# One group in 42 of a gather fetched row by row by SyncE, at byte offsets from registers

## The chip, the cores and the metric

The kernel runs on one core of one Trainium2 chip. A core has a matrix engine (TensorE, PE in the profile), a vector engine (VectorE, DVE), a scalar engine (ScalarE, ACT), a general engine (GpSimd, POOL) and a synchronising engine (SyncE, SP), each with its own list of instructions, and 16 DMA engines that all of them share. The metric is the device time of one execution in microseconds (us), the median of several runs.

## The reference

The kernel scores 16384 users of a recommender. There are 50001 items. For every item two attention steps over 32 neighbours give two vectors of 32 numbers; with a looked-up row of 64 they make the item's row of 128. Each user has a history of 100 items and one target item:

```python
a_sus = _neighbor_attn(E_in, near_full)        # 50001 x 32: softmax over 32 neighbours
a_inf = _neighbor_attn(E_out, near_full)
h = concat([E_hist[history], a_sus[history], a_inf[history]])   # 16384 x 100 x 128
t = concat([E_tgt[target], a_inf[target], a_sus[target]])       # 16384 x 128
z = relu(einsum('bld,hd->blh', h * t[:, None, :], W1) + b1)
exp_A = exp(einsum('blh,h->bl', z, W2[0])) * ((history != target[:, None]) & (history != 0))
attn = exp_A / sum(exp_A, axis=-1, keepdims) ** 0.5
s = sum(h * attn[..., None])                   # one number over everything
out = sigmoid(cosine(s broadcast, t))
```

The row of `h` for every user and every history position, 1,638,400 rows of 128 numbers, has to be looked up by index. That look-up is what the change is about.

## The kernel before

The kernel has two stages, one after the other.

The first stage computes the item rows. It takes the items in 391 sub-tiles of 128 (23 blocks of 17; the names `NITER`, `NSUB`), gathers the 32 neighbours of each with 32 indirect DMAs on POOL (line 136, tile `v`), does the attention on DVE and ACT, and writes the rows to two tables in memory: `table` with the history version and `ttab` with the target version. A row of `table` has `W` = 129 numbers, 516 bytes: the sum of the row first, so that it need not be computed again, then the 128 numbers.

The second stage, the user stage, takes the 16384 users in `UC` = 128 chunks of 128, one user to a partition. The 100 history positions of a chunk are worked in `NG` = 25 groups of `LG` = 4 positions. The steps of the loop are numbered `s` = 25 c + g, 3200 in all. The functions are:

- `history_of(i)` (line 290): SP loads the history numbers of four chunks (`BSUB`) into a tile `hidx`; four such tiles exist (`u_in`).
- `target_rows(c)` (line 294): one indirect DMA on POOL gathers the 128 target rows of a chunk; `target_work(c)` (line 304) turns them with PE and builds the mask on DVE.
- `gather(s)` (line 325): four indirect DMAs on POOL (line 332) gather the four rows of each of the 128 users, one position at a time, into a tile `h` of 128 x 4 x 129; there are `HBUF` = 20 of these.
- `turn(s)` (line 342): PE turns the four 128 x 128 blocks (line 346) into a PSUM tile `hT_ps`, of which there are three.
- `times_target(s)` (line 348): DVE multiplies by the target rows (line 351) and copies the four row sums aside (line 354).
- `hidden(s)`, three steps later: PE multiplies by `w1T` (line 363), ACT applies relu (line 365).
- `scored(s)`, six steps later: PE multiplies by the one row of W2 (line 372), adding up the 25 groups of a chunk in one PSUM tile.
- `kept`, `turned_back`, `weights`, `ended`: once for each chunk, exponentials, mask and sums.

In this stage the order of the work on all five engines is the order in which the program calls these functions (`tc.manual_schedule`). Each engine runs its own instructions in that order and waits on semaphores for what it needs. POOL can run ahead of PE by as many groups as there are `h` tiles. SP has 32 history lists to load in this stage and, at the end, one result to write. A `history_of` call stands at the third chunk of a list and loads the next one:

```python
if g == 0 and c % BSUB == 2 and 0 < c // BSUB and c // BSUB + 1 < UC // BSUB:
    history_of(c // BSUB + 1)
```

An indirect DMA of POOL takes one index per partition from a tile on the core and fetches 128 rows. A DMA of SP, as used before, moves a block whose place in memory is fixed when the program is built.

Of the kernel before, what the change touches and what calls it, by code (L numbers as in the profile page):

```python
# [10 lines left out]
F32 = mybir.dt.float32  # L11
I32 = mybir.dt.int32
U8 = mybir.dt.uint8
E = mybir.EngineType
AF = mybir.ActivationFunctionType
ALU = mybir.AluOpType
AX = mybir.AxisListType

P = 128
ITEMS = 50001  # L20
# [21 lines left out]
UC = B // P  # L42
BSUB = 4
LG = 4
NG = L // LG
W = 1 + D
LAG = 3
HBUF = 20

@with_exitstack
def kernel(
# [13 lines left out]
    nc = tc.nc  # L67
# [8 lines left out]
    table = dram.tile([ROWS, W], F32, name="table")  # L76
# [3 lines left out]
    ident = const.tile([P, P], F32, name="ident")  # L80
# [25 lines left out]
    with (  # L106
# [7 lines left out]
        its = {}  # L114
# [15 lines left out]
        def gather(s):  # L130
            it, j = divmod(s, NSUB)
            nidx = its[it][0]
            v = n_v.tile([P, K, 2, G], F32, name="v")
            subs[s].update(v=v)
            for k in range(K):
                nc.gpsimd.indirect_dma_start(  # L136
                    out=v[:, k].rearrange("p t d -> p (t d)"),
                    out_offset=None,
                    in_=egeo,
                    in_offset=bass.IndirectOffsetOnAxis(ap=nidx[:, j, k : k + 1], axis=0),  # L140
                )
# [128 lines left out]
    with (  # L270
# [2 lines left out]
        tc.tile_pool(name="u_in", bufs=4) as u_in,  # L273
        tc.tile_pool(name="u_t", bufs=3) as u_t,
        tc.tile_pool(name="u_h", bufs=HBUF) as u_h,
        tc.tile_pool(name="u_x", bufs=6) as u_x,
        tc.tile_pool(name="u_z", bufs=6) as u_z,
        tc.tile_pool(name="u_s", bufs=3) as u_s,
# [8 lines left out]
        users, hists = {}, {}  # L287
        rows, got, hT, xT, z = {}, {}, {}, {}, {}

        def history_of(i):  # L290
            hists[i] = u_in.tile([P, BSUB, L], I32, name="hidx")
            nc.sync.dma_start(hists[i], hist_v[i])

        def target_rows(c):
            t = u_t.tile([P, D], F32, name="t")
            nc.gpsimd.indirect_dma_start(  # L296
                out=t,
                out_offset=None,
                in_=ttab[0:ITEMS, :],
                in_offset=bass.IndirectOffsetOnAxis(ap=tidx[:, c : c + 1], axis=0),  # L300
            )
            users[c] = {"t": t, "hidx": hists[c // BSUB][:, c % BSUB, :]}

        def target_work(c):
            u = users[c]
            t = u["t"]
            tT_ps = ps_t.tile([P, LG, P], F32, name="hT_ps")
            nc.tensor.transpose(tT_ps[:, 0, :], t, ident)  # L308
            tT = u_t.tile([D, 1, P], F32, name="tT")
            nc.vector.tensor_copy(tT[:, 0, :], tT_ps[:, 0, :])  # L310
            u["tT"] = tT
            nc.vector.tensor_reduce(tsum[:, c : c + 1], t, AX.X, ALU.add)
            junk = u_t.tile([P, D], F32, name="junk")
            nc.scalar.activation(junk, t, AF.Square, accum_out=tsq[:, c : c + 1])
            keep = u_s.tile([P, L], F32, name="keep")
            idf = u_s.tile([P, L], F32, name="idf")
            nc.vector.tensor_copy(idf, u["hidx"])
            nc.vector.tensor_scalar(keep, idf, 0.0, None, ALU.not_equal)
            nc.vector.scalar_tensor_tensor(
                keep, idf, tidf[:, c : c + 1], keep, ALU.not_equal, ALU.mult  # L320
            )
            u["keep"] = keep
            u["hsum"] = u_s.tile([P, L], F32, name="hsum")

        def gather(s):
            c, g = divmod(s, NG)
            rows[s] = u_h.tile([P, LG, W], F32, name="h")
            got[s] = []
            for q in range(LG):
                l = g * LG + q  # L330
                got[s].append(
                    nc.gpsimd.indirect_dma_start(  # L332
                        out=rows[s][:, q, :],
                        out_offset=None,
                        in_=table,
                        in_offset=bass.IndirectOffsetOnAxis(
                            ap=users[c]["hidx"][:, l : l + 1], axis=0
                        ),
                    )
                )  # L340

        def turn(s):
            c, g = divmod(s, NG)
            hT[s] = ps_t.tile([P, LG, P], F32, name="hT_ps")
            for q in range(LG):
                nc.tensor.transpose(hT[s][:, q, :], rows[s][:, q, 1:W], ident)  # L346

        def times_target(s):
            c, g = divmod(s, NG)
            xT[s] = u_x.tile([D, LG, P], F32, name="xT")  # L350
            nc.vector.tensor_tensor(  # L351
                xT[s], hT.pop(s), users[c]["tT"].to_broadcast([D, LG, P]), ALU.mult
            )
            copy = nc.vector.tensor_copy(  # L354
                users[c]["hsum"][:, g * LG : (g + 1) * LG],
                rows.pop(s)[:, :, 0:1].rearrange("p q o -> p (q o)"),
            )
            for one in got.pop(s):
                tc.declare_no_dep(copy.ins, one.ins, reason="TensorE has read the row")

        def hidden(s):
            z_ps = ps_z.tile([HID, LG, P], F32, name="z_ps")
            nc.tensor.matmul(z_ps, w1T, xT.pop(s), start=True, stop=True)  # L363
            z[s] = u_z.tile([HID, LG, P], F32, name="z")
            nc.scalar.activation(z[s], z_ps, AF.Relu, bias=b1_sb)  # L365

        def scored(s):
            c, g = divmod(s, NG)
            of = z.pop(s)
            if g == 0:  # L370
                users[c]["turned"] = ps_s.tile([NG, LG * P], F32, name="turned")
            nc.tensor.matmul(  # L372
                users[c]["turned"],
                w2_row[:, NG - 1 - g : 2 * NG - 1 - g],
                of.rearrange("h q p -> h (q p)"),
                start=g == 0,
                stop=g == NG - 1,
            )

        def kept(c):  # L380
            users[c]["by_g"] = u_s.tile([NG, LG * P], F32, name="by_g")
            nc.scalar.copy(users[c]["by_g"], users[c]["turned"])

        def turned_back(c):
            users[c]["score"] = ps_1.tile([P, LG, NG], F32, name="score")
            for q in range(LG):
                nc.tensor.transpose(
                    users[c]["score"][:, q, :],
                    users[c]["by_g"][:, q * P : (q + 1) * P],
                    ident[0:NG, 0:NG],  # L390
                )

        def weights(c):
            users[c]["ea"] = u_s.tile([P, L], F32, name="ea")
            nc.scalar.activation(
                users[c]["ea"].rearrange("p (g q) -> p q g", q=LG), users[c]["score"], AF.Exp
            )

        def ended(c):
            u = users.pop(c)  # L400
            ea = u["ea"]
            nc.vector.tensor_tensor(ea, ea, u["keep"], ALU.mult)  # L402
            nc.vector.tensor_reduce(den[:, c : c + 1], ea, AX.X, ALU.add)  # L403
            nc.vector.tensor_tensor(ea, ea, u["hsum"], ALU.mult)  # L404
            nc.vector.tensor_reduce(num[:, c : c + 1], ea, AX.X, ALU.add)  # L405
# [3 lines left out]
        history_of(1)  # L409
        target_rows(0)  # L410
        target_work(0)
        for s in range(last + 2 * LAG + 8):
            c, g = divmod(s, NG)
            if s < last:
                if g == 0 and c % BSUB == 2 and 0 < c // BSUB and c // BSUB + 1 < UC // BSUB:
                    history_of(c // BSUB + 1)
                if g == 5 and c + 1 < UC:
                    target_rows(c + 1)
                gather(s)
                turn(s)  # L420
                times_target(s)
            if 0 <= s - LAG < last:
                hidden(s - LAG)
            if 0 <= s - 2 * LAG < last:
                scored(s - 2 * LAG)
            if s < last and g == 15 and c + 1 < UC:
                target_work(c + 1)
            done, left = divmod(s - 2 * LAG - NG, NG)
            if 0 <= done < UC and left == 0:
                kept(done)  # L430
            if 0 <= done < UC and left == 2:
                turned_back(done)
            if 0 <= done < UC and left == 4:
                weights(done)
            if 0 <= done < UC and left == 6:
                ended(done)

    with (
# [12 lines left out]
        s = f_s.tile([P, 1], F32, name="s")  # L451
# [72 lines left out]
```

## Time and profile before

| What | Value |
| --- | --- |
| median of 3 runs | 36178.12 us |
| lowest and highest | 36170.38 and 36182.2 us |
| span of the profiled execution | 31861.9 us |
| median less that span | 4316.2 us |
| first stage in the span | 0 to about 15692 us |
| user stage in the span | about 15692 to 31862 us |
| instructions | 106268 |
| history gathers on POOL | 12800 |
| target gathers on POOL | 128 |
| neighbour gathers on POOL, first stage | 12512 |

The profile is of one execution. For it the page gives the span, from the first instruction's start to the last one's end, and no time beside it; what the runs take over the span is not in the trace. POOL, PE, DVE, ACT and SP are as above; PEld is PE's loading of weights, which overlaps its products. In the page's groups, the number after "|" is the busy time in us, then the mean of one instruction in nanoseconds, then the idle time of that engine just before these instructions with what ended most of it. "issue" means that the engine waited for nothing that the profile shows. For an instruction that issues a DMA on SP the duration is the time that SP is held; "to landing" is the time until the data has arrived. L332 is line 332 of the kernel above.

### The profile page before, as it was taken

To read this page: it belongs to the slowest core of one execution; us is meant where nothing else is said; L and a number is where in the kernel's file an instruction comes from. 1 tells how busy PE (TensorE), PEld (TensorE's weight loads), DVE (VectorE), ACT (ScalarE), POOL (GpSimd) and SP (SyncE) were. 2 spreads that over 40 slices of the span, in tenths; PEclk is the share of its full clock that TensorE was granted. 3 is DMA by queue.
4 is the path that set the end of the run, shared out by engine and by line. 5 is a ranking of instruction groups with operands and counts; after the bars stand their busy time and mean duration, and the time that the engine had idled before them with its cause. 6 is when DMAs were issued, how large, how long until landed. Compare 5 with 4: busy or idle time off the path is not lost.

```text
span 31861.9 us, 106268 instructions
## 1 busy us (share of the span) xinstructions
PE 11868.8 (37%) x26243; PEld 3178.4 (10%) x26243; DVE 6716.4 (21%) x11111; ACT 2745.2 (9%) x6067; POOL 24005.6 (75%) x25446
## 2 busy tenths in 40 slices
PE   0000000000000000000277777777777777777777
PEld 0000000000000000000011111111111111111111
DVE  2222222222222222222211111111111111111111
ACT  0000000000000000000011111111111111111111
POOL 7777777777777777777777777777777777777777
PEclk9999999999999999999988888888888888888888
DMA  2111111111111111111122222222222222222222
GB/s 50 30 30 30 30 31 33 30 30 30 30 31 33 30 30 30 30 31 31 37 54 54 54 54 54 54 54 54 54 54 54 54 54 54 54 54 54 54 53 52
DMA packets 1027971, 1362.44 MB, mean 43 GB/s; under 512 B 559904, under 2 KB 614432, under 8 KB 1027360
## 3 DMA queue, kind: packets, MB, share of 16 engines
q0 software_dynamic: 814080, 1265.42, 19.7%
q10 hardware_dynamic: 151056, 51.51, 1.0%
q1 hardware_dynamic: 62224, 38.72, 0.5%
q8 instruction: 217, 3.56, 0.0%
q14 instruction: 394, 3.23, 0.0%
HBM read 1315.31 MB, written 51.50 MB: 43 GB/s over the span
## 4 chain that ended last, share of the span: by engine, by line
POOL 56%; issue 27%; DMA 9%; PE 7%; DVE 1%; POOLq 0%; ACT 0%; ACTq 0%; SPq 0%; DVEq 0%
POOL v L136 35%; POOL h L332 21%; DMA h<-table,hidx 6%; PE turned L372 3%; DMA v<-in_egeo_dram,nidx 3%; PE z_ps L363 3%; PE hT_ps L346 1%; POOL t L296 0%; DVE xT L351 0%; DVE ea L404 0%; DVE den L403 0%; DVE num L405 0%; DVE ea L402 0%; DVE hsum L354 0%; DMA table<-row 0%
## 5 line engine op out<-in xcount | busy, mean ns | idle before, releaser
L332 POOL DMA_INDIRECT h<-table,hidx x12800 | 12080.4, 944 | 3901.8 <-issue 3587.3
L136 POOL DMA_INDIRECT v<-in_egeo_dram,nidx x12512 | 11803.8, 943 | 3860.2 <-issue 3723.3
L308 PE MATMUL hT_ps<-ident,t 128*128 128x128 f32 x128 | 46.7, 365 | 15689.8 <-DMA hidx<-in_history_dram 15689.8
L346 PE MATMUL hT_ps<-ident,h 128*128 128x128 f32 x12800 | 3926.4, 350 | 4284.2 <-DMA h<-table,hidx 4186.4
L351 DVE TENSOR_TENSOR xT<-hT_ps,tT 128x512 f32<-128x512 f32 x3200 | 2213.9, 692 | 13113.0 <-PE hT_ps L346 13109.7
L372 PE MATMUL turned<-z,w_row 128*25 128x512 f32 x6400 | 4560.1, 805 | 0.0
L363 PE MATMUL z_ps<-xT,w1T 128*128 128x512 f32 x6400 | 4300.2, 761 | 0.0
L365 ACT ACTIVATE z<-z_ps,b_sb 128x512 f32<-128x512 f32 x3200 | 2199.7, 687 | 13823.9 <-PE z_ps L363 13823.9
L153 DVE TENSOR_TENSOR big<-v,own_ps 128x2048 f32<-128x2048 f32 x391 | 897.9, 2296 | 11251.8 <-DMA v<-in_egeo_dram,nidx 11251.5
L346 PEld LDWEIGHTS hT_ps<-ident,h 128*128 128x128 f32 x12800 | 1779.4, 154 | 9334.4 <-DMA h<-table,hidx 5701.4
L308 PEld LDWEIGHTS hT_ps<-ident,t 128*128 128x128 f32 x128 | 19.2, 150 | 15842.7 <-issue 15841.9
L180 ACT ACTIVATE ex<-sc,top 128x32 f32<-128x32 f32 x782 | 227.7, 291 | 15155.2 <-DVE top L172 15142.5
L363 PEld LDWEIGHTS z_ps<-xT,w1T 128*128 128x128 f32 x6400 | 1343.1, 255 | 3.1 <-ACT z L365 3.1
L194 DVE TENSOR_TENSOR big<-v,ex 128x1024 f32<-128x1024 f32 x782 | 960.6, 1228 | 355.5 <-ACT ex L180 342.0
L163 DVE TENSOR_REDUCE sc<-big 128x64 f32<-128x2048 f32 x391 | 896.4, 2293 | 13.4
L207 DVE TENSOR_REDUCE att<-big 128x64 f32<-128x2048 f32 x391 | 895.8, 2291 | 0.0
L372 PEld LDWEIGHTS turned<-z,w_row 128*25 128x25 f32 x6400 | 458.8, 115 | 3323.6 <-issue 3323.6
L354 DVE COPY hsum<-h 128x4 f32<-128x4 f32 x3200 | 528.5, 165 | 0.0
L296 POOL DMA_INDIRECT t<-ttab,tidx x128 | 120.8, 943 | 66.0 <-issue 37.8
L180 ACT ACTIVATION_READ_ACCUMULATOR ex<-sc,top 128x1 f32 x782 | 145.8, 186 | 0.0
L310 DVE COPY tT<-hT_ps 128x128 f32<-128x128 f32 x128 | 37.4, 292 | 262.4 <-PE hT_ps L308 262.4
L214 DVE TENSOR_TENSOR row<-att,tot 128x64 f32<-128x64 f32 x391 | 88.2, 226 | 13.3
(55 smaller groups left out, 1008.1 us busy)
## 6 DMA issues: line engine op xcount, KB each, us to landing
h<-table,hidx POOLq DMA_INDIRECT x12800, 2.6
v<-in_egeo_dram,nidx POOLq DMA_INDIRECT x12512, 2.4
table<-row ACTq DMA_DIRECT2D x22, 1096.5 KB, 13.4
own<-in_egeo_dram SPq DMA_DIRECT2D x23, 544.0 KB, 4.0
row<-in_ehist_dram SPq DMA_DIRECT2D x23, 544.0 KB, 4.9
ttab<-in_etgt_dram ACTq DMA_DIRECT2D x1, 12500.0 KB, 54.2
ttab<-row ACTq DMA_DIRECT2D x22, 544.0 KB, 4.6
hidx<-in_history_dram SPq DMA_DIRECT2D x32, 200.0 KB, 2.5
```

Of the source, the lines that this page charges most:

```text
L136: nc.gpsimd.indirect_dma_start(out=v[:, k].rearrange("p t d -> p (t d)"), out_offset=None, in_=egeo, in_offset=bass.IndirectOffsetOnAxis(a ...
L153: nc.vector.tensor_tensor(prod.rearrange("p k t d -> p k (t d)"), v.rearrange("p k t d -> p k (t d)"), subs[s]["own"].to_broadcast([P, K, ...
L163: nc.vector.tensor_reduce(sc.rearrange("p t k -> p k t"), subs[s]["prod"], AX.X, ALU.add)
L194: nc.vector.tensor_tensor(subs[s]["wv"][:, t].rearrange("p d k -> p k d"), subs[s]["v"][:, :, t, :], subs[s]["ex"][0][:, t, :] .rearrange( ...
L207: nc.vector.tensor_reduce(att, subs[s]["wv"], AX.X, ALU.add)
L332: nc.gpsimd.indirect_dma_start(out=rows[s][:, q, :], out_offset=None, in_=table, in_offset=bass.IndirectOffsetOnAxis(ap=users[c]["hidx"][: ...
L346: nc.tensor.transpose(hT[s][:, q, :], rows[s][:, q, 1:W], ident)
L351: nc.vector.tensor_tensor(xT[s], hT.pop(s), users[c]["tT"].to_broadcast([D, LG, P]), ALU.mult)
L354: copy = nc.vector.tensor_copy(users[c]["hsum"][:, g * LG : (g + 1) * LG], rows.pop(s)[:, :, 0:1].rearrange("p q o -> p (q o)"),)
L363: nc.tensor.matmul(z_ps, w1T, xT.pop(s), start=True, stop=True)
L365: nc.scalar.activation(z[s], z_ps, AF.Relu, bias=b1_sb)
L372: nc.tensor.matmul(users[c]["turned"], w2_row[:, NG - 1 - g : 2 * NG - 1 - g], of.rearrange("h q p -> h (q p)"), start=g == 0, stop=g == N ...
```

## The change

One in `EACH` = 42 groups of the user stage is no longer gathered by POOL. These are the steps `s` with `s % 42 == 41`, except for the last 25 steps; there are 75. `gather(s)` returns at once for them, and a new function `fetch(s)` brings their rows instead, with SP:

- DVE copies the group's 128 x 4 item numbers as floats (`fidf`), PE turns them to 4 x 128 in a PSUM tile of the `hT_ps` pool, and DVE multiplies by 516 and writes them as integers (`fat`): byte offsets into `table`, one row of the tile to a history position.
- SP loads these offsets into registers, `RUN` = 16 at a time (32 loads to a group), and issues one DMA for each row of the table, 516 bytes, to its partition and position in a tile `fh` (512 to a group).

A new pool `u_f` holds two of each of these tiles, apart from the 20 `h` tiles. Two fetches are called before the loop; after that a fetched step, once it has been turned and multiplied, calls the fetch for the step 84 later. In the built program the DMAs of SP use eight completion semaphores in turn, and each DMA waits for the one eight before it. The four DMAs of a gather are no longer there for these steps, and the copy of the row sums waits for the fetch's DMAs. The history lists are loaded earlier: at the first chunk of a list, the list after the next one.

```diff
+EACH = 42
+RUN = 16
...
+        tc.tile_pool(name="u_f", bufs=2) as u_f,
...
+        def fetched(s):
+            return s % EACH == EACH - 1 and s + NG < UC * NG
+
+        table_flat = table.rearrange("(o n) d -> o (n d)", o=1)
+
+        def fetch(s):
+            c, g = divmod(s, NG)
+            idf = u_f.tile([P, LG], F32, name="fidf")
+            nc.vector.tensor_copy(
+                idf, hists[c // BSUB][:, c % BSUB, g * LG : (g + 1) * LG]
+            )
+            at_ps = ps_t.tile([P, LG, P], F32, name="hT_ps")
+            nc.tensor.transpose(at_ps[0:LG, 0, :], idf, ident)
+            at = u_f.tile([LG, P], I32, name="fat")
+            nc.vector.tensor_scalar(at, at_ps[0:LG, 0, :], 4.0 * W, None, ALU.mult)
+            rows[s] = u_f.tile([P, LG, W], F32, name="fh")
+            got[s] = []
+            for q in range(LG):
+                for p in range(0, P, RUN):
+                    _, vals = nc.values_load_multi_w_load_instructions(
+                        at[q : q + 1, p : p + RUN],
+                        engines=[E.SP],
...
+                    for i, v in enumerate(vals):
...
+                        nc.sync.dma_start(
+                            rows[s][p + i : p + i + 1, q, :], table_flat[:, ds(v // 4, W)]
+                        )
+
         def gather(s):
             c, g = divmod(s, NG)
+            if fetched(s):
+                return
...
+        fetch(EACH - 1)
+        fetch(2 * EACH - 1)
         for s in range(last + 2 * LAG + 8):
             c, g = divmod(s, NG)
             if s < last:
-                if g == 0 and c % BSUB == 2 and 0 < c // BSUB and c // BSUB + 1 < UC // BSUB:
-                    history_of(c // BSUB + 1)
+                if g == 0 and c % BSUB == 0 and c // BSUB + 2 < UC // BSUB:
+                    history_of(c // BSUB + 2)
                 if g == 5 and c + 1 < UC:
                     target_rows(c + 1)
                 gather(s)
                 turn(s)
                 times_target(s)
+                if fetched(s) and fetched(s + 2 * EACH):
+                    fetch(s + 2 * EACH)
```

More of the change, by code (lines that the diff above doesn't have):

```diff
@@ L323, in target_work @@
             u["hsum"] = u_s.tile([P, L], F32, name="hsum")
+        def fetched(s):
[18 more added lines that the diff above has]
+                        engines=[E.SP],
+                        min_val=0,
+                        max_val=(ITEMS - 1) * 4 * W,
+                        skip_runtime_bounds_check_because="an item's number, times its row's bytes",
+                    )
+                    for i, v in enumerate(vals):
+                        v = v.with_bounds(
+                            min_val=0,
+                            max_val=(ITEMS - 1) * 4 * W,
+                            guaranteed_mod_val=0,
+                            out_of_modulus=4 * W,
+                        )
+                        nc.sync.dma_start(
+                            rows[s][p + i : p + i + 1, q, :], table_flat[:, ds(v // 4, W)]
+                        )
         def gather(s):
             c, g = divmod(s, NG)
+            if fetched(s):
+                return
             rows[s] = u_h.tile([P, LG, W], F32, name="h")
```

## The prediction

> **What bounds the kernel now.** I read the page's busy times first, then its slices over time, then the chain that ended last, and then the two stages apart in a table of two windows (columns: length, then busy us and instruction count of PE, PEld, DVE, ACT, POOL, then granted clock, DMA share, GB/s).
>
> ```profile
> span 31861.9 us, 106268 instructions
> PE 11868.8 (37%) x26243; PEld 3178.4 (10%) x26243; DVE 6716.4 (21%) x11111; ACT 2745.2 (9%) x6067; POOL 24005.6 (75%) x25446
> PE   0000000000000000000277777777777777777777
> POOL 7777777777777777777777777777777777777777
> POOL 56%; issue 27%; DMA 9%; PE 7%; DVE 1%; POOLq 0%; ACT 0%; ACTq 0%; SPq 0%; DVEq 0%
> L332 POOL DMA_INDIRECT h<-table,hidx x12800 | 12080.4, 944 | 3901.8 <-issue 3587.3
> ...
> 15692.00:31862.00 16170.00, 11868.38 (x26242) 3178.20 (x26242) 2752.60 (x7565) 2332.24 (x3720) 12201.11 (x12928) 0.81 0.25 54
> ```
>
> POOL shows only seven tenths in every slice, yet it is the bound: the chain gives it 56% and another 27% to "issue", time in which it waited for nothing the profile shows. The timeline of POOL shows how a single gather stands to the next.
>
> ```profile
> 20002.36 0.94 POOL L332 DMA_INDIRECT h<-table,hidx  x1 [0.30 <-issue]
> 20003.61 0.94 POOL L332 DMA_INDIRECT h<-table,hidx  x1 [0.30 <-issue]
> ...
> L332 POOL DMA_INDIRECT h<-table,hidx x12800: 940/944/1040, 15694.9 to 31833.3; - x197
> DMA to landing us min/median/max: 2.4/2.6/4.0
> ```
>
> One starts every 1.25 us, 0.944 busy and 0.30 of issue. From the first gather's start, 15694.9, to the last one's end, 31833.3 + 0.9 = 31834.2, there are 16139.3 us and, by the window, 12928 POOL instructions (12800 history gathers, 128 target gathers): 1.2484 us each, without a hole. So the user stage costs what its number of gathers costs. PE, the next engine, is busy 11868 of 16170 us, 73%, and waits for rows the rest. SP does next to nothing:
>
> ```profile
> SPq L292 <- DMA h<-table,hidx: 14109.1, 84, 506.4
> ```
>
> Nearly all of its stage is one wait for buffers of the history list.
>
> **What is removed.** With EACH = 42 the fetched groups are 41, 83, ..., 3149, that is 75 of 3200. Four gathers each make 300 gathers that POOL no longer runs: 300 x 1.2484 = 374.5 us. As POOL has no holes, these come off the path whole, provided that SP delivers each fetched group before PE wants it.
>
> **What SP must now do.** Between two fetched groups POOL runs 41 x 4 gathers and 42/25 target gathers, 165.7 x 1.2484 = 206.8 us. In that time SP issues 512 DMAs of one row (516 bytes) and 32 register loads of 16 values. The allowance is 206.8/512 = 0.404 us a row, loads included. Whether the change gains or loses hangs on this figure, and the trace has only relatives of both instructions, from SP's own rows (nanoseconds min/median/max):
>
> ```profile
> L292 SPq EVENT_SEMAPHORE  x148: 17/28/1356, 15667.0 to 29818.4; - x148
> L292 SPq DMA_DIRECT2D hidx<-in_history_dram x32: 327/328/617, 15692.2 to 29819.7; - x32
> DMA to landing us min/median/max: 2.4/2.5/3.8
> ...
> L119 SPq DMA_DIRECT2D nidx<-in_near_dram x23: 333/334/1703, 2.2 to 14306.1; - x23
> ...
> L124 SPq DMA_DIRECT2D row<-in_ehist_dram x23: 550/551/648, 55.0 to 14406.6; - x23
> ...
> L85 SPq DMA_DIRECT2D b_sb<-in_b_dram x1: 384/384/384, 0.7 to 0.7; - x1
> DMA to landing us min/median/max: 2.0/2.0/2.0
> ...
> 2051.99 0.34 SPq L119 DMA_DIRECT2D nidx<-in_near_dram  x1
> 2052.38 0.42 SPq L121 DMA_DIRECT2D own<-in_egeo_dram  x1
> ```
>
> *A row's issue.* A history list, 128 pieces of 1600 bytes, holds SP 0.328 us; the item lists, also 128 pieces, 0.334; 2176 pieces 0.551. So 2048 more pieces add 0.217, about 0.1 ns each: nearly all is a fixed price, and one piece instead of 128 saves 0.013. The next issue follows 0.39 us after the start of the former, a gap of 0.055. I take 0.328 - 0.013 + 0.055 = 0.37 us, 189.4 us for 512. The address now comes from a register, which no row shows; the upper end is the dearest of the 128-piece issues in steady state, 0.42, with its gap: 0.47. For the lower end I use the completions. In the built program each row's DMA waits for the semaphore of the row eight before it, so no row can cost less than an eighth of a landing: 2.5/8 = 0.31 by the history list. Between 0.31 and 0.47 I keep 0.37, since the row it is nearest to in kind, 0.328, repeats 32 times within a nanosecond at its median.
>
> *A register load.* No row shows one. Lower end: one sequencer-only instruction, 0.028 us. Upper end: a whole memory round trip like a landing, 2.5 us. I take 16 values at 0.028 each, 0.45 us, because the nearest thing SP does without data movement is that semaphore row; 32 x 0.45 = 14.3 us. [...]
>
> *The sum for one fetched group.* T = 189.4 + 14.3 = 203.7 us, against 206.8: it fits, by 1.5%. The ends are 512 x 0.31 + 32 x 0.03 = 160 and 512 x 0.47 + 32 x 2.5 = 321.
>
> *If it doesn't fit.* Two groups are under way in two buffers, so SP works without a pause and the 75 fetches take 75 T; behind the last one 50 groups remain, of which POOL, 20 buffers ahead, has 30 left (150 us) and PE 50 x 3.7 = 185 us, with some 28 us of ending: the stage would be 75 T + 215 us. POOL's own limit after the change is 16170 - 374.5 = 15795.5. The two meet at T = 207.7. The gain is gone at T = 212.7, and each us more costs 75 us.
>
> **What is added elsewhere.** Per fetched group DVE makes two operations of 128x4 and 4x128 elements and PE one transpose. PE's is like its 350 ns row:
>
> ```profile
> L346 PE MATMUL hT_ps<-ident,h 128*128 128x128 f32 x12800 | 3926.4, 350 | 4284.2 <-DMA h<-table,hidx 4186.4
> L351 DVE TENSOR_TENSOR xT<-hT_ps,tT 128x512 f32<-128x512 f32 x3200 | 2213.9, 692 | 13113.0 <-PE hT_ps L346 13109.7
> L354 DVE COPY hsum<-h 128x4 f32<-128x4 f32 x3200 | 528.5, 165 | 0.0
> ```
>
> PE stands in order, so it waits until DVE has done the product (0.69), the sums (0.165) and the copy (0.165): about 1.0 + 0.35 us, 75 times, 101 us. I cost it at nothing: PE idles 16170 - 11868 = 4302 us of the stage, 57 in each period, and POOL is 20 groups (100 us) ahead through its buffers. Without that cover it would be 101 us. The 38400 rows are 19.8 MB that the gathers moved before; DMA engines are at a share of 0.25 by the window, so contention is nothing as well. Behind SP's waits stand the history lists: a list may be held up by one fetch, some 204 us, but it is now asked for two lists (200 groups, 1000 us) before its first use, so nobody waits.
>
> **The sum.** Span 31861.9 - 374.5 = 31487. The span is 4316.2 us below the median of the runs, 36178.12, and the page doesn't show where those lie. I take them as untouched: 36178.1 - 374.5 = 35804. If they grow and shrink with the gathers, the gain is 374.5 x 36178/31862 = 425 and the time 35753.
>
> **Rivals.** (1) *SP becomes the bound through its register loads: slower.* For it: the load is in no row, the room is 3 us in 207, and a load that must fetch from memory may stop SP for a round trip. It decides from (212.7 - 189.4)/32 = 0.73 us a load. At 1.5 us, T = 237, the stage is 17990 and the time 37998; at 2.5 us, T = 269, it is 20390 and 40398. Against it: the values lie in on-chip memory, and the load is one instruction for sixteen. [...]
>
> (2) *The window of eight completions becomes the bound: slower.* At a landing of 3.3 us it passes 0.404 us a row; at the longest landing of the gathers, 4.0, a row costs 0.5, T = 270, and the time is 40470. Against it: the median is 2.5 and the smallest transfers take 2.0.
>
> (3) *No change.* The 4316 us outside the span may mean that unprofiled executions are bound by something other than POOL in this stage, PE at a lower clock (0.81 here) being the nearest; then fewer gathers are worth nothing: 36178. Break-even at T near 212.7 falls here too. Against it: PE would have to be slower by a third.
>
> **How the numbers follow.** Forecast and partial gains 0.58, rival 1 0.24, rival 2 0.08, rival 3 0.10. About half of the slower cases, those up to T = 237, end below 38000; those beyond (0.16) are left out. The range is 35700, some 50 us under the fully scaled gain, to 38000, and holds 0.84. The forecast's own range is 35700 to 35900. A change of under 0.2%, 72 us, could not be told from none: faster 0.58, same 0.10, slower 0.32.
>
> **What would show it.** POOL: 12500 history gathers, still 1.25 us apart without holes in the user stage. SP: an issue near 0.33 us for each row, one every 0.37; a load of 0.45; and pauses of some us at each fetched group, waiting for the buffer. The prediction is wrong if SP has no pauses, PE waits for "fh" and POOL's gathers show holes behind its buffers, or if the loads are above 0.7 us.

## The result, and the profile after

The changed kernel takes 44838.9 us (median of 4 runs, 44779.6 to 44840.0) against 36178.1: 1.239 times as long, 95% interval 1.2373 to 1.2408. The prediction was 35804 us, a gain of 1%. Before, here, is the profile that the prediction read. The first fence has the page of the changed kernel: span, busy time of each engine, two rows of its slices, and two of its groups.

```profile
span 44837.6 us, 187004 instructions
PE 10144.7 (23%) x26318; PEld 3169.3 (7%) x26318; DVE 6685.8 (15%) x11261; ACT 2701.7 (6%) x6067; POOL 25264.4 (56%) x25146
PE   0000000000000001333333333333333333333333
POOL 7777777777777776444444444444444444444444
L374 POOL DMA_INDIRECT h<-table,hidx x12500 | 11822.8, 946 | 15265.7 <-PE z_ps L405 8806.4
L388 PE MATMUL hT_ps<-ident,fh 128*128 128x128 f32 x300 | 128.5, 428 | 9816.4 <-DMA fh<-table 9730.4
```

POOL, at seven tenths throughout the user stage before, is at four tenths now, and PE at three instead of seven. POOL's idle time before its gathers has grown from 3901.8 to 15265.7 us, most of it waiting for PE; PE in turn waits 9730 us for `fh`, the rows that SP fetches. The table of two windows (columns as in the prediction's) and three waits say the same of the stage: 27306 us instead of 16170. (A second profile of the kernel before, in the first experiment, has the time of the runs. By it the stage took 18704 us, POOL idled 6379.2 us before these gathers, and PE was at five tenths. From there to 27306 are 8602 of the 8661 us lost.)

```profile
0.00:17531.00 17531.00, 1.64 (x4) 0.53 (x4) 3966.24 (x3557) 413.29 (x2349) 13323.01 (x12521) 1.00 0.15 28
17531.00:44837.00 27306.00, 10143.05 (x26314) 3168.80 (x26314) 2719.58 (x7705) 2288.41 (x3718) 11941.36 (x12626) 0.66 0.15 32
```

```profile
PE hT_ps L388 <- DMA fh<-table: 9730.4, 219, 58.6
POOL h L374 <- PE z_ps L405: 8806.4, 176, 133.4
...
SPq L361 <- DMA fh<-table: 191.2, 369, 1.4
```

SP is the bound. Counted over its 38400 rows in the trace, a fetch takes 358.9 us on the average from its first row to its last (345 to 465), and the next one begins 1.9 us later; 75 times 360.8 is 27060 of the stage's 27306 us. SP itself waits for the completion of its own rows for 191 us in all. So the 359 us are its own instructions. These are the rows of the tiles `fh` and `fat`, in nanoseconds min/median/max:

```profile
L361 SPq MOVE fh<-table x38400: 1/29/1410, 17531.6 to 44594.1; - x199
L361 SPq DMA_DIRECT2D fh<-table x38400: 1/228/1405, 17531.7 to 44594.2; - x199
...
L347 SPq TENSOR_LOAD <-fat x2400: 3/1228/1432, 17530.4 to 44588.0; - x185
```

The medians are cheap: 0.228 us for an issue, 0.029 for a register move that the build puts beside each row, 1.228 for a load of sixteen registers. From start to start a row costs 0.323 us at the median and a load 1.281: 512 x 0.323 + 32 x 1.281 = 206.4 us. By the prediction's allowance of 206.8 that would just have fitted. The other 152 us of each fetch lie in the upper half of these distributions, and the timeline shows when. The columns are start, length and, at the end, how many rows SP issued in that time; first SP in two stretches in which POOL is silent, then SP and POOL in one in which it gathers:

```profile
25040.06 6.09 SPq L361 DMA_DIRECT2D fh<-table  x15
...
25120.89 5.11 SPq L361 DMA_DIRECT2D fh<-table  x16
...
25200.13 6.31 SPq L361 DMA_DIRECT2D fh<-table  x4
25199.77 0.95 POOL L374 DMA_INDIRECT h<-table,hidx  x1 [0.30 <-issue]
25201.02 0.94 POOL L374 DMA_INDIRECT h<-table,hidx  x1 [0.30 <-issue]
25202.27 0.95 POOL L374 DMA_INDIRECT h<-table,hidx  x1 [0.30 <-issue]
```

Fifteen or sixteen rows in five to six us beside a silent POOL, four beside a gathering one. The gathers keep their distance of 1.25 us.

### The profile page after: what moved, and what is told of

Read it like the earlier page. It is cut to its first block, busy times and chain, and to the rows that moved or that the text cites. A ratio compares the mean times of both kernels' runs of the same rounds, so it can differ in the third digit from the quotient of the medians.

```text
span 44837.6 us, 187004 instructions
## 1 busy us (share of the span) xinstructions
PE 10144.7 (23%) x26318; PEld 3169.3 (7%) x26318; DVE 6685.8 (15%) x11261; ACT 2701.7 (6%) x6067; POOL 25264.4 (56%) x25146
## 5 line engine op out<-in xcount | busy, mean ns | idle before, releaser
L374 POOL DMA_INDIRECT h<-table,hidx x12500 | 11822.8, 946 | 15265.7 <-PE z_ps L405 8806.4
L138 POOL DMA_INDIRECT v<-in_egeo_dram,nidx x12512 | 13319.6, 1065 | 4175.9 <-issue 4078.7
L414 PE MATMUL turned<-z,w_row 128*25 128x512 f32 x6400 | 4084.6, 726 | 0.0
L388 PE MATMUL hT_ps<-ident,h 128*128 128x128 f32 x12500 | 2314.6, 313 | 522.1 <-DVE xT L393 376.5
L388 PE MATMUL hT_ps<-ident,fh 128*128 128x128 f32 x300 | 128.5, 428 | 9816.4 <-DMA fh<-table 9730.4
L388 PEld LDWEIGHTS hT_ps<-ident,h 128*128 128x128 f32 x12500 | 1497.8, 156 | 3629.4 <-issue 2821.5
L405 PEld LDWEIGHTS z_ps<-xT,w1T 128*128 128x128 f32 x6400 | 1186.5, 232 | 7037.7 <-ACT z L407 6068.3
L196 DVE TENSOR_TENSOR big<-v,ex 128x1024 f32<-128x1024 f32 x782 | 960.7, 1228 | 355.4 <-ACT ex L182 217.8
```

The costliest lines, as they stand in the source:

```text
L138: nc.gpsimd.indirect_dma_start(out=v[:, k].rearrange("p t d -> p (t d)"), out_offset=None, in_=egeo, in_offset=bass.IndirectOffsetOnAxis(a ...
L196: nc.vector.tensor_tensor(subs[s]["wv"][:, t].rearrange("p d k -> p k d"), subs[s]["v"][:, :, t, :], subs[s]["ex"][0][:, t, :] .rearrange( ...
L374: nc.gpsimd.indirect_dma_start(out=rows[s][:, q, :], out_offset=None, in_=table, in_offset=bass.IndirectOffsetOnAxis(ap=users[c]["hidx"][: ...
L414: nc.tensor.matmul(users[c]["turned"], w2_row[:, NG - 1 - g : 2 * NG - 1 - g], of.rearrange("h q p -> h (q p)"), start=g == 0, stop=g == N ...
```

## The experiments

For all of them the time of a fetch is counted over SP's rows as above, and a time of the kernel before is from runs on the same chip beside them.

**Where the 4316 us lie.** The kernel before, profiled once more.

> The kernel before, unchanged, for its trace beside the others. Theory: the 4316 us by which its runs exceed the span of its first profile lie inside the execution; as the first stage of the changed kernel, which is the same in both, took 17519 us where the first profile of the kernel before had 15692, the span will be near 36176 us, the first stage near 17500 and the user stage near 18650. Rival: they lie around the span, and the span is again near 31862 us with a first stage of 15692.

The time was 36200.3 us and the span 36198.5. The windows of this profile:

```profile
0.00:17494.00 17494.00, 0.45 (x1) 0.18 (x1) 3950.10 (x3535) 411.73 (x2340) 13202.66 (x12518) 1.00 0.13 28
17494.00:36198.00 18704.00, 10043.88 (x26242) 3144.18 (x26242) 2737.47 (x7576) 2297.31 (x3727) 12199.02 (x12929) 0.73 0.19 46
...
L292 SPq DMA_DIRECT2D hidx<-in_history_dram x32: 3/328/1397, 17524.9 to 33806.8; - x32
```

The time is inside the span: the first stage takes 17494 us and not 15692, the user stage 18704 and not 16170, 1.447 us for each of 12929 POOL instructions. The profile from which the prediction was made is of an execution that the timed ones are not like. It had its gathers without holes and SP's list issues at 327 to 617 ns; here, with the same median, single issues take up to 1397. In this execution the gathers of the first stage stand 1.25 us apart for 285 us and then lose their beat:

```profile
282.45 0.95 POOL L136 DMA_INDIRECT v<-in_egeo_dram,nidx  x1 [0.30 <-issue]
...
284.97 1.09 POOL L136 DMA_INDIRECT v<-in_egeo_dram,nidx  x1 [0.30 <-issue]
286.37 1.10 POOL L136 DMA_INDIRECT v<-in_egeo_dram,nidx  x1 [0.30 <-issue]
287.77 1.79 POOL L136 DMA_INDIRECT v<-in_egeo_dram,nidx  x1 [0.30 <-issue]
```

**A third of the fetches, with room to spare.**

```diff
-EACH = 42
+EACH = 126
-        fetch(2 * EACH - 1)
-                if fetched(s) and fetched(s + 2 * EACH):
-                    fetch(s + 2 * EACH)
+                if fetched(s) and fetched(s + EACH):
+                    fetch(s + EACH)
```

> One group in 126 fetched instead of one in 42, with one fetch under way at a time (25 groups, 100 gathers fewer). SP then has 126 groups of time, about 620 us, for 512 rows. Both theories expect that this is enough, and a gain of 100 gathers, 125 to 145 us (36030 to 36050). They differ in how long a fetch takes. Theory 'slowed beside POOL': in the changed kernel SP issued 2.4 rows a us while POOL stood still and 0.6 to 1.2 while it worked; here POOL always works, so a fetch takes about 510 us and a row about 1.0 us. Theory 'own price': a row costs SP what it cost on the average there, 0.705 us, whatever POOL does, so a fetch takes 361 us.

36313.5 us against 36185.5, 1.0034 times (1.0022 to 1.0047). SP now pauses 176.6 us between fetches and nobody waits for it, but a fetch takes 565.9 us, not less than before: POOL, no longer held up, gathers beside it all the time. And 100 gathers fewer, worth 100 x 1.447 = 145 us, gave no gain; the time is 128 us longer. What the fetches cost when nobody waits for them can't be read from that. Sets of runs differ by as much: the kernel before has a median of 36185.5 us beside this run and of 36321.0 beside later ones, and the last run below, with all its gathers and no fetch, has a user stage of 18816 us where this one has 18820.

**The same with little work on PE.** Only the first group of a chunk goes through the products. The lines below are the difference to the run before, without the line that closes PE's sum after that one group.

```diff
-                hidden(s - LAG)
-            if 0 <= s - 2 * LAG < last:
+                if (s - LAG) % NG == 0:
+                    hidden(s - LAG)
+                else:
+                    xT.pop(s - LAG)
+            if 0 <= s - 2 * LAG < last and (s - 2 * LAG) % NG == 0:
```

> As the kernel with one group in 126, but hidden and scored are run only for the first of the 25 groups of each chunk, so PE does little beside its turning (24 of 25 of the hidden layer's products and relus are left out; the result is not the reference's). Theory 'POOL alone is worst': in the changed kernel SP issued 0.56 rows a us where POOL worked and PE stood, 1.23 where both worked; with PE mostly idle a fetch then takes 700 to 900 us, more than the 620 us it has, and SP holds the stage up: 25 x 800 us and more, 37500 to 41000 us in all. Rival 'only POOL counts': PE's work changes nothing, a fetch takes as long as with the products, and the time is that of the kernel with one group in 126.

A fetch took 753.4 us, as the first theory had it: with PE out of the way SP is slower, not faster. Counted by gathers the two are nearer. In the run before this one 387 gathers start between a fetch's first row and its last, here 508: each costs SP (565.9 - 206.4)/387 = 0.93 us there and (753.4 - 206.4)/508 = 1.08 here. Why a gather costs more here was not tried. The whole took 36689 us and not 37500 or more; that part of the expectation was summed wrongly, since 25 fetches of 758 us are 18950, no more than the stage takes anyway.

**Only the row issues, no registers.** The changed kernel, with 512 rows at places fixed in the program.

```diff
-                    _, vals = nc.values_load_multi_w_load_instructions(
-                        at[q : q + 1, p : p + RUN],
...
-                    for i, v in enumerate(vals):
+                    for i in range(RUN):
                         nc.sync.dma_start(
-                            rows[s][p + i : p + i + 1, q, :], table_flat[:, ds(v // 4, W)]
+                            rows[s][p + i : p + i + 1, q, :],
+                            table[(s * 13 + q * P + p + i) : (s * 13 + q * P + p + i) + 1, :],
```

> As the changed kernel (one group in 42), but SP fetches 512 rows at fixed places of the table instead of the users' rows: no register loads, no register moves, no bounds from registers; the number and size of the DMAs stay (the wrong rows are fetched, so the result is not the reference's). Theory 'SP's instructions are slowed one by one beside POOL, whatever they are': with one instruction for a row instead of two and a sixteenth, a fetch takes about half of 361 us, near 180 us, under the 207 us it has, and the time falls 300 gathers under the kernel before, near 35800. Rival 'the DMAs themselves are slowed beside POOL' (their descriptors or completions): a fetch stays well above 207 us, and the time stays above 40000.

Between the two: 38510 us, a fetch 275.9 us, a row 0.294 us apart at the median and 0.54 at the mean. Loads and moves are 359 - 276 = 83 us of a fetch. The issue alone is held as well, since 512 x 0.294 would be 151 us.

**The fetches from the start.**

```diff
-        NT = NITER * NSUB
-        load(0)
-        for s in range(NT + 3):
...
+    for to in (flat_t, flat_u):
+        for n, given in enumerate((flat_h, flat_e)):
+            nc.scalar.dma_start(
+                to[n * N1 : (n + 1) * N1].rearrange("(a b) -> a b", a=1024),
+                given.rearrange("(a b) -> a b", a=1024),
+            )
...
```

> The changed kernel without its first stage: table and ttab are filled by flat copies of the given features, so the outputs are not the reference's. The user stage then begins within the first 150 us. In the kernel before, the gathers of the first stage stand 1.25 us apart for 285 us, and only then do stretches with slow ones begin. Theory A (something that builds up over the first 285 us, whatever engine works, holds SyncE back in steps of 0.70 us afterwards): rows issued before about 285 us stand 0.323 us apart although GpSimd gathers beside them, so the first fetch takes 206 to 260 us, and the later ones 345 to 465 as in the changed kernel. Theory B (GpSimd's gathers hold SyncE back whenever they run): the first fetch already takes 340 us or more, its rows 0.6 to 0.7 us apart beside a working GpSimd. The whole by both: 75 x 360.8 + 240 = 27300, plus about 150, some 27450 us, against 44838.9 with the first stage; A would give up to 200 us less.

Theory B. The first fetch began at 169 us and took 466.4, the next ones 368 and 355; the whole took 27851 us, some 400 more than by either theory, at 365.8 us from one fetch to the next. The stretch after 200 us, before the beat is lost anywhere, and one at 560 us, in which POOL is silent:

```profile
198.96 0.94 POOL L233 DMA_INDIRECT h<-table,hidx  x1 [0.30 <-issue]
200.21 0.94 POOL L233 DMA_INDIRECT h<-table,hidx  x1 [0.30 <-issue]
201.46 0.94 POOL L233 DMA_INDIRECT h<-table,hidx  x1 [0.30 <-issue]
...
197.71 12.59 SPq L220 DMA_DIRECT2D fh<-table  x5
...
559.92 2.16 SPq L220 DMA_DIRECT2D fh<-table  x7
```

Five rows in 12.6 us beside gathers that stand perfectly regular, seven in 2.2 us beside none. The hold does not need 285 us. It is not there at once either. In the changed kernel gathers begin again 74 times after 15 us or more without one and then stand less than 1.4 us apart for at least 18 us. Counted over these 74, SP issues 2.6 rows a us in the first 2 us, 1.45 from 4 to 6, 0.95 from 6 to 8 and 0.47 from 16 to 18. So the hold builds up over some ten us of gathers, and a price for one gather is an average.

**The gathers taken away.** The changed kernel, POOL gathering one group in 25.

```diff
+            if g != 0:
+                rows[s] = kept_rows[c]
+                return
             rows[s] = u_h.tile([P, LG, W], F32, name="h")
+            kept_rows[c] = rows[s]
```

> The changed kernel in which GpSimd gathers only the first of a chunk's 25 groups and the other groups of the chunk use that tile again (three fetches that would fall on a first group are left out, 72 remain), so the scores are not the reference's. TensorE, VectorE and ScalarE do their work as before. Theory (GpSimd's gathers are what slows SyncE): a fetch falls from 359 to 206 to 230 us, the fetches follow each other at 210 to 235 us, the user stage takes about 72 x 222 = 16000 and the whole 33000 to 34500 us. Rival (any engine's work slows SyncE alike): the fetch stays above 280 us and the whole above 37500.

A fetch took 212.6 us (210 to 228), one followed the other at 214.8, and the whole took 33143 us, all three inside the theory's bounds. PE, DVE and ACT did all their work beside SP; they hold it back by 6 us at most (212.6 - 206.4).

**POOL busy with something else.** As the last one, but with POOL at work in the groups that it doesn't gather.

```diff
                 rows[s] = kept_rows[c]
+                for _ in range(LG):
+                    nc.gpsimd.memset(filler, 0.0)
```

> As the run with few gathers (only the first group of a chunk gathered, its tile used again by the others, so the scores are not the reference's; a fetch fell there to 212.6 us), but in each of the other groups GpSimd writes zeros four times into a tile of 128x512 that nothing reads: it works again in nearly every group, on something that transfers nothing. Theory A (the gather holds SyncE back, by the descriptors or transfers that it makes): the fetch stays at 213 to 235 us and the whole at 33100 to 34500 us. Theory B (any instruction of a working GpSimd holds SyncE back): the fetch takes 290 us or more and the whole more than 38500.

Theory A, and even a little below its bounds of 213 and 33100: 210.7 us a fetch, 32999 us in all. In the same ten us POOL writes 18 tiles and SP issues 25 rows:

```profile
19999.87 10.41 POOL L375 MEMSET filler<- 128x512 f32 x18
20000.44 9.74 SPq L363 DMA_DIRECT2D fh<-table  x25
```

**What of a gather it is.** As the run with few gathers, but the other groups' gathers are made into a tile that nobody reads, with rows of 64 bytes in one kernel and 16 full rows in the other.

```diff
                 rows[s] = kept_rows[c]
+                small = u_h.tile([P, LG, 16], F32, name="small")
+                for q in range(LG):
+                    l = g * LG + q
+                    nc.gpsimd.indirect_dma_start(
+                        out=small[:, q, :],
+                        out_offset=None,
+                        in_=table_short,
+                        in_offset=bass.IndirectOffsetOnAxis(
+                            ap=users[c]["hidx"][:, l : l + 1], axis=0
+                        ),
+                    )
```

and between this one and the second:

```diff
-                small = u_h.tile([P, LG, 16], F32, name="small")
+                small = u_h.tile([P, LG, W], F32, name="small")
-                        out=small[:, q, :],
+                        out=small[0:16, q, :],
-                        in_=table_short,
+                        in_=table,
-                            ap=users[c]["hidx"][:, l : l + 1], axis=0
+                            ap=users[c]["hidx"][0:16, l : l + 1], axis=0
```

> As the run with few gathers (the groups after a chunk's first use its tile again, so the scores are not the reference's; a fetch took 212.6 us there), but GpSimd makes the gathers of these groups too, of 128 rows each, into a tile that nothing reads, and each row has 16 values (64 bytes) and not 129 (516 bytes). Nobody paces these gathers, they can stand close. Theory A (the instruction itself, or the list of 128 rows that it makes, holds SyncE back, whatever the rows' size): the fetch takes 350 to 1500 us and the whole 42000 us or more. Theory B (the bytes that are moved hold SyncE back): the fetch stays at 213 to 260 us, the whole at 33000 to 36500.

> As the run with short rows, but each of these gathers takes 16 full rows of 516 bytes and not 128 (the scores are not the reference's). Theory A1 (what holds SyncE is the list of rows, so an eighth of it holds it an eighth as long): the fetch takes 213 to 300 us, the whole 33000 to 39500. Theory A2 (the instruction holds SyncE for as long as GpSimd is at it, and that is about the same for 16 rows): the fetch takes more than 350 us, as with short rows, the whole 42000 or more.

A and A2: a fetch took 408.5 and 411.7 us, the whole 47248 and 47476. An eighth of the bytes and an eighth of the rows changed nothing. The gathers, first with short rows, then with few (ns min/median/max), and two stretches of SP in the first, without and with them:

```profile
L377 POOL DMA_INDIRECT small<-table,hidx x12000: 938/944/1795, 17536.7 to 46763.1; - x197
...
20050.47 5.11 SPq L363 DMA_DIRECT2D fh<-table  x16
...
20249.83 6.30 SPq L363 DMA_DIRECT2D fh<-table  x3
20249.92 0.94 POOL L377 DMA_INDIRECT small<-table,hidx  x1 [0.30 <-issue]
20251.16 0.94 POOL L377 DMA_INDIRECT small<-table,hidx  x1 [0.30 <-issue]
```

```profile
L376 POOL DMA_INDIRECT small<-table,hidx x12000: 832/837/1798, 17538.3 to 46986.1; - x197
```

It is the gather as such: 16 rows take POOL 0.837 us where 128 take 0.944, and hold SP as long. Whether what counts in it is the instruction or the report of its end, these two runs can't tell. In the changed kernel there are 12628/75 = 168.4 gathers to a fetch (targets included), so each costs SP (358.9 - 206.4)/168.4 = 0.91 us on the average; with the unpaced short and few rows, 12640/72 = 175.6 to a fetch, it is 1.15 and 1.17. The fetches of the short-row run lie beside very different numbers of gathers, from none to 514, and that settles what the time hangs on: over its 72 fetches the time is 206.6 us plus 1.15 us for each gather that starts during the fetch (correlation 0.999). The 206.6 are the 206.4 that SP's own rows add up to where nothing holds them.

**Does it work on another engine, and in the other direction?** The kernel before with twelve tiny copies a group on ACT.

```diff
...
+            if s < last:
+                for _ in range(12):
+                    nc.scalar.copy(tiny, ones[:, 0:1])
```

> The kernel before with twelve copies of 128x1 elements on ScalarE added to each of the 3200 groups: 38400 small instructions that move next to nothing, make no transfer, and stand on an engine that is mostly idle. Theory (each instruction of any engine takes from something that all engines share, as the 2400 loads and 38400 moves of the fetches seem to do): the added 38400 slow the gathers of GpSimd, and the time goes up by 150 us or more, to 36350 to 36900. Rival (only transfers, or SyncE beside GpSimd, disturb each other): within 0.2% of 36185.

36792.8 us against 36321.0, 1.0129 times (1.0099 to 1.0158): inside the theory's range. 38400 instructions that transfer nothing cost 472 us, 12 ns each, and the windows put them into the user stage alone. But they need not have slowed the gathers for that. The copies are held themselves, in steps of some 0.7 us, though the engine waits for nothing but its own last copy, and so ACT has become the path: the chain that ended last gives it 42% of the span, 36% in these copies, where it had 3% in the second profile of the kernel before. That a small instruction off the path costs the other engines something is therefore not shown. The last four lines show that the hold sets in late on ACT too: after a pause in the gathers twelve copies pass in 2.63 us, though POOL gathers regularly.

```profile
ACT 42%; POOL 33%; issue 20%; another core or an unknown queue 4%; PE 0%; DMA 0%; POOLq 0%; DVE 0%; SPq 0%; ACTq 0%
L429 ACT COPY tiny<-ones 128x1 f32<-128x1 f32 x38400 | 7315.2, 190 | 9982.3 <-ACT tiny L429 6351.5
...
25000.30 0.19 ACT L429 COPY tiny<-ones 128x1 f32<-128x1 f32 x1 [1.21 <-ACT tiny L429]
25001.01 0.19 ACT L429 COPY tiny<-ones 128x1 f32<-128x1 f32 x1 [0.52 <-ACT tiny L429]
25001.73 0.19 ACT L429 COPY tiny<-ones 128x1 f32<-128x1 f32 x1 [0.53 <-ACT tiny L429]
25003.14 0.19 ACT L429 COPY tiny<-ones 128x1 f32<-128x1 f32 x1 [1.22 <-issue]
...
25012.65 2.63 ACT L429 COPY tiny<-ones 128x1 f32<-128x1 f32 x12
25012.49 0.94 POOL L333 DMA_INDIRECT h<-table,hidx  x1 [4.55 <-issue]
25013.73 0.94 POOL L333 DMA_INDIRECT h<-table,hidx  x1 [0.31 <-issue]
25014.98 0.95 POOL L333 DMA_INDIRECT h<-table,hidx  x1 [0.30 <-issue]
```

**The lists alone.** The kernel before, with only the history lists loaded earlier.

```diff
-                if g == 0 and c % BSUB == 2 and 0 < c // BSUB and c // BSUB + 1 < UC // BSUB:
-                    history_of(c // BSUB + 1)
+                if g == 0 and c % BSUB == 0 and c // BSUB + 2 < UC // BSUB:
+                    history_of(c // BSUB + 2)
```

> The kernel before with only the other part of the change, the lists of history positions loaded two chunks earlier, and nothing fetched by SyncE. All theories: the load has ended long before its use in both, so no change, 36185 within 0.2% (36110 to 36260). If it were slower by more, the earlier lists and not the fetches would carry part of the 8660 us.

36317.3 us against 36321.0 (0.9988 to 1.0011 times): nothing, as expected. All of the loss belongs to the fetches.

## Why the prediction was wrong

**The step that failed is "the sum for one fetched group", T = 203.7 us.** The prediction added up SP's instructions from rows in which SP ran as if alone, and took it that they cost the same beside POOL. In the profile that it read this was so, as far as its rows go: list loads beside gathers took 0.328 us at the median, and the gathers kept their beat. In the timed executions it is so only without gathers: 210.7 and 212.6 us where POOL gathers next to nothing. Beside gathers T is 358.9 us, above even the upper end, 321, because each gather takes 0.91 us of SP's time on the average in this kernel. A register move is held like a row's issue: where at least 12 gathers begin in the 16 us before, both take 0.697 us at the median, and where none does, 0.029 and 0.228. No term of the sum, and no rival, had in it that SP's instructions are held beside gathers, and the time, 44838.9 us, lies above what every rival gave.

Even without the hold the forecast stood on an edge. From one fetch to the next it was then 212.8 and 214.8 us, against the prediction's own break-even of 212.7. By the pace of the timed executions, 165.7 x 1.447 = 240 us, it would have fitted.

Step by step:

- *A row's issue, 0.37 us.* 0.323 where nothing holds it, move and gap included; inside the bounds. The move that the build puts before each row was not counted: 38400 more instructions, 29 ns each.
- *A register load, 0.45 us.* 1.28 from start to start; inside the bounds, but 2.8 times the value taken. The two errors cancel, which is luck: 512 x (0.323 - 0.37) = -24 us and 32 x (1.28 - 0.447) = +27. In the trace a load of sixteen takes 1228 ns at the median, 1228/16 = 77 ns a register.
- *If it doesn't fit: 75 T + 215 us.* Right. With the measured T it gives 27133 us; the stage took 27306, and 75 x 1.9 us between the fetches are most of the difference.
- *"The 4316.2 us are taken as untouched."* The reason was missing, and it mattered: they are in both stages, in slower gathers and in holes between them. The execution in that profile was 12% shorter than the timed ones, and its prices were not theirs.
- *300 gathers fewer, 374.5 us.* By the timed executions 300 x 1.447 = 434 us at the most. None of it shows: in the run with a third of the fetches and no wait for SP, a third of it was to be gained, and the time was 128 us longer.
- *Added work at nothing.* Open. In the same run the missing 145 us and the 128 us of loss would make 11 us for each of its 25 fetches, against 4 x 1.447 = 5.8 that one saves. But sets of runs of one kernel differ by 136 us (36185.5 and 36321.0), so that price is not shown. At the one rarer spacing that was run there is no gain.
- *Rival 1, SP bound through its loads.* The right engine and sign, by another mechanism. A load passed the 0.73 us from which it was to decide, but the cheaper row made that up; with loads and moves gone altogether (rows at fixed places) the kernel still lost 2325 us.
- *Rival 2, the window of eight completions.* It fell: SP waits 191 us for them in 27306. *Rival 3, no change,* fell too, though its premise held in part: the timed executions are not the ones of the profile, and their gathers cost 1.447 us and not 1.248.
- *What would show it wrong:* SP without pauses, PE waiting for `fh`, and holes in POOL behind its buffers. All three are there, and the loads are above 0.7 us.

## What to carry to other kernels

A second queue with idle time was not a free resource here (a fetch took 210.7 and 212.6 us beside a POOL that gathers next to nothing, 358.9 in the changed kernel): before work is moved to one, ask what the engine that it will run beside does to it, and price the work from rows in which the two overlap. If the span of a profile and the time of the runs differ by more than a few us, find out where the difference lies before anything is summed, since prices from the one may not hold in the other. Count the instructions, too, and not only the bytes (here 1024 issues and moves for 4 gathers saved): each of them can be held, as rows and moves were (0.697 us at the median where gathers stand close), and 38400 small copies on ACT, which had 3% of the chain that ended last, raised its share to 42%.

## What the runs showed of the hardware that was not expected

- Once POOL had run indirect gathers for some ten us, SP's instructions beside them were held in steps of about 0.70 us (in the changed kernel 0.47 rows a us after 16 us of gathers, 2.6 in the first two). From 200 to 220 us in the run without a first stage, register moves took 0.70 us and not 0.029, and a row 2.8 us and not 0.323. Copies on ACT in the user stage were held in like steps; that it was the gathers there too was not tried apart. The gathers didn't give way in that stretch: 16 in 20 us beside 7 rows. POOL's memsets (0.524 us each) held nothing: 210.7 us a fetch. Gathers of 128 rows of 64 bytes (408.5 us a fetch), of 128 rows of 516 (358.9) and of 16 rows of 516 (411.7) all did.
- About 285 us into an execution of the kernel before, gathers begin to be slow too (0.95 us becoming 1.1 to 1.8), with nothing in the program changing. From start to start they then stand 1.25 or 1.40 us apart, or 1.96 and 2.10, which is 0.70 more. In the first profile of the same kernel one of 25440 gathers takes more than 1.05 us, and the median distance is 1.249.
- What engines share here is not settled. A register move makes no transfer and is held all the same (0.697 us at the median), so transfers of its own don't explain it. One candidate, a guess, is the recording of the profile itself. In the first profile of the kernel before, where no hold is seen, the trace keeps 656 semaphore events per 50 us of the first stage, at the median. In the changed kernel's it keeps 559 in the first 50 us, and from 100 us on 71 at the median to the first stage's end: one in 0.70 us, about the step of the holds. In the runs with short and with few rows, too, 50 us full of gathers keep 72 at the median, and 50 us beside memsets 246 to 479. In the first profile the eight semaphores of the 25440 gathers have 406981 landings, 16 to a gather. No run here shows that the recording stopped an engine. Every run of the experiments has its span on record, within 3 us of its time. So an execution without recording was not tried, and whether it would show this loss is open.
